# Mamba steps that alternate over both halves of the channels, with a gather in two 128x64 products and DRAM reads that repeat 64 rows

## The chip, the cores and the metric

The kernel runs on one core of one Trainium2 chip. The metric is the device time of one execution in microseconds (us); before the change it is 8173.62 us, the median of three runs (8168.15 to 8188.78). A core has five engines that run on their own queues: PE (matrix products, into the accumulator memory PSUM), DVE (VectorE), ACT (ScalarE), POOL (GpSimd) and SP, which only issues transfers. Transfers are carried out by 16 DMA engines.

## The reference

Four layers run one after the other on an image x of 2 x 64 channels x 96 x 96, all in float32. Layer 0 is attention over the 9216 points of each image. Layer 1 is a depthwise and a pointwise convolution and one Mamba block over the 9216 points as one sequence. Layer 2 runs four Mamba blocks: forward and backward along one image axis, then forward and backward along the other, over sequences of 96. Layer 3 is a 3x3 filter whose taps are computed from the image's means. The change is in the Mamba block, of which this is the core:

```python
dt, Bm, Cm = jnp.split(dbc, [DT_RANK, DT_RANK + D_STATE], axis=-1)
dt = jax.nn.softplus(jnp.einsum('blr,dr->bld', dt, dt_proj_w) + dt_proj_b)
A = -jnp.exp(A_log)
dA = jnp.exp(dt[..., None] * A)
dBx = dt[..., None] * Bm[:, :, None, :] * xc[..., None]

def step(hc, inp):
    dA_t, dBx_t, C_t = inp
    hc = hc * dA_t + dBx_t
    y = jnp.einsum('bds,bs->bd', hc, C_t)
    return (hc, y)
...
ys = (ys + xc * Dp) * jax.nn.silu(z)
```

There are 128 inner channels d and 16 states s: 2048 recurrences run beside each other along the time l.

## The kernel before, in words

**Units and steps.** The work of layers 1 and 2 is cut into 120 units of 768 columns of time (`CH`): 24 in layer 1 (12 for each image, one after the other in time, with the last state carried on in `u.carry`), and 96 in layer 2 (8 sequences of 96 in each, forward or backward, no carry). A unit has 16 steps (`STEPS`), since 128 partitions hold 128 of the 2048 recurrences at a time (16 of them for all 768 columns, or 32 half as long), and so there are 1920 steps.

**Which recurrence lies where.** In step n, partition p works on state p // 8 and on channel (p + 8n) mod 128. After 16 steps each channel has met all 16 states. To bring the channels to their partitions, a unit writes its 128 rows of dt and dt*x (`u.both`, 1536 columns) to DRAM twice, one below the other (`step_write`, L824, two transfers of 768 KB), into `rows` of 256 x 1536. A step then reads 128 rows from row 8n on (`read`): that is a turn by 8n.

**Two forms of a step.** In layer 1 a step reads one transfer of 768 KB (L842), for all 768 columns of one group of channels n. In layer 2 (`u.paired`) a step takes one half of the time, 384 columns, for two neighbouring groups 2m and 2m + 1, side by side in the free dimension, and reads them with two transfers of 384 KB (L847). The rest of a step:

- `decay` on ACT: exp(rate * dt) into `h`, one activation of 768 columns (L853) or two of 384 (L857), since the rate differs between groups.
- `shared` on PE: B for all partitions (L866), into a bank that all steps of the unit (or of a half of its time) read.
- `inputs` on DVE: dt*x times B into a `place` in PSUM (L872, L877). In layer 2 those of two steps come together, ahead of an even step.
- `scan` on DVE: the recurrence along 768 columns (L884 with the carried state, L890 without: there a decay of zero at the start of each sequence resets it). POOL then multiplies by C (L886, L893), and in layer 1 copies the last state (L885).
- `gather` on PE: a 128x128 matrix of zeros and ones (`t.gather[n]`) adds the 128 rows of `h` to their channels. Layer 1 adds columns 0 to 383 into the bank `low0` and the others into `low1`; layer 2 adds both groups into `low1` (L910), 3840 products in all, each standing as two records in the profile. The product with `direct` (L907), ahead of the first, puts the term with Dp there.

**The order.** `run` writes the order out by hand. In iteration n SP gets the reads of step n + 5 (`READ`), ACT the decay of step n + 3, DVE the inputs and scan of step n, PE the gather of a step two back (`lates`), and then those parts of earlier or later units whose offsets in `PIECES` fall on n: norm, convolution, gate, dt, C ahead of the unit, and the reading of y and the output projection behind it. `step_write` stands at -8, so between the reads of steps -3 and -2 of its unit. `spread`, the tile that a read fills, has six buffers, and `h` nine. `y_half` and `y_read` (L915, L919, L923) copy the finished halves of y from PSUM. Between the last unit of layer 1 and the first of layer 2 the form changes, and a branch gathers and reads out y at once (`u.drained`).

**Tables.** `mamba_tables` builds the matrices of the gather (`pair`, two identities side by side, of which 16 windows are taken) and, with `turned`, what `mamba_weights` needs to put the rates of each step in its order. This runs during attention.

Of the kernel before, what the change touches and what calls it, by code (L numbers as in the profile page):

```python
# [523 lines left out]
def mamba_tables(k, pool):  # L524

    nc = k.nc
    G = P // 8
    t = SimpleNamespace()  # L530

    t.member = pool.tile([P, 8], FP, name="member")
    nc.vector.reduce_sum(t.member, k.ident.rearrange("p (g i) -> p i g", i=8), axis=AX.X)
    t.group = pool.tile([P, 2, G], FP, name="group")
    for j in range(2):
        nc.vector.reduce_sum(t.group[:, j], k.ident.rearrange("p (g i) -> p g i", i=8), axis=AX.X)

    t.turned = pool.tile([P, G, G], FP, name="turned")
    two = t.group.rearrange("p j g -> p (j g)")
    for n in range(G):  # L540
        nc.vector.tensor_copy(t.turned[:, n], two[:, G - n : 2 * G - n])

    pair = pool.tile([P, 2, P], FP, name="pair")
    nc.vector.tensor_copy(pair, k.ident.unsqueeze(1).to_broadcast([P, 2, P]))
    pair = pair.rearrange("p j c -> p (j c)")
    t.gather = [pair[:, P - 8 * n : 2 * P - 8 * n] for n in range(G)]

    t.centre = pool.tile([P, P], FP, name="centre")
    nc.vector.tensor_sub(t.centre, k.ident, k.mean_c)
    return t  # L550
# [8 lines left out]
def mamba_weights(k, w, pool, product, tables, i):  # L559
# [15 lines left out]
    p = product(tables.placed.rearrange("p s i -> p (s i)"), tables.group[:, 0], P, G)  # L575
# [38 lines left out]
class Mamba:  # L614
# [14 lines left out]

    STEPS = P // 8  # L630
# [3 lines left out]
    def __init__(self, k, tables, wk, dram, ps, ps_m):  # L634
        self.k, self.nc, self.t = k, k.nc, tables
        self.wk, self.dram, self.ps_m = wk, dram, ps_m


        self.places = [self.wide(ps.tile([P, 2 * NB], FP, name=f"place{i}")) for i in range(2)]
        self.low = [ps.tile([P, NB], FP, name=f"low{i}")[:, :HALF] for i in range(2)]  # L640
# [141 lines left out]
    def step_read(self, u):  # L782
        nc = self.nc

        u.both = self.work("dtu", 2 * CH, bufs=1)
        order = "p (j a t) -> p a j t" if u.paired else "p (a j t) -> p a j t"
        both = u.both.rearrange(order, a=2, j=2)
        u.dt, u.e = both[:, 0], both[:, 1]
        u.kept = self.by_half(self.work("kept", bufs=1))
        p = self.by_half(u.p)  # L790
        nc.scalar.activation(u.e, p, AF.Abs, bias=u.w.dt_b)
        nc.scalar.activation(u.dt, p, AF.Relu, bias=u.w.dt_b)
# [28 lines left out]
    def step_write(self, u):  # L821
        u.rows = self.dram.tile([2 * P, 2 * CH], FP, tag="rows", name="rows")
        for j in range(2):
            self.nc.sync.dma_start(out=u.rows[j * P : (j + 1) * P], in_=u.both)  # L824
# [10 lines left out]
    def paired(self, step):  # L835
        half, m = divmod(step, self.STEPS // 2)
        return half, (2 * m, 2 * m + 1)

    def read(self, u, step):
        u.dtu[step] = self.work("spread", 2 * CH, bufs=6)  # L840
        if not u.paired:
            self.nc.sync.dma_start(out=u.dtu[step], in_=u.rows[8 * step : 8 * step + P])  # L842
            return
        half, groups = self.paired(step)
        for q, n in enumerate(groups):
            row = u.rows[8 * n : 8 * n + P, bass.ts(half, CH)]
            self.nc.sync.dma_start(out=u.dtu[step][:, bass.ts(q, CH)], in_=row)  # L847

    def decay(self, u, step):

        h = u.h[step] = self.work("h", bufs=9)
        if not u.paired:
            self.nc.scalar.activation(h, u.dtu[step][:, :CH], AF.Exp, scale=u.w.rates[:, step : step + 1])  # L853
            return
        for q, n in enumerate(self.paired(step)[1]):
            dt = u.dtu[step][:, q * CH : q * CH + HALF]
            self.nc.scalar.activation(h[:, bass.ts(q, HALF)], dt, AF.Exp, scale=u.w.rates[:, n : n + 1])  # L857

    def shared(self, u, half=0):

        if u.paired:
            sides, halves = [self.low[0]], [half]
        else:
            (sides, u.B), halves = self.places[1], range(2)
        for j, p in zip(halves, sides):
            self.nc.tensor.matmul(p, lhsT=u.w.bc[0], rhs=u.xc[:, bass.ts(j, HALF)], start=True, stop=True)  # L866

    def inputs(self, u, step):

        if not u.paired:  # L870
            u.bx = self.places[0][1]
            self.nc.vector.tensor_mul(u.bx, u.dtu[step][:, CH:], u.B)  # L872
            return
        bx = self.places[step % 2][1].rearrange("p (q t) -> p q t", q=2)
        x = u.dtu[step].rearrange("p (q a t) -> p q a t", q=2, a=2)[:, :, 1]
        B = self.low[0].unsqueeze(1).to_broadcast([P, 2, HALF])
        self.nc.vector.tensor_mul(bx, x, B)  # L877

    def scan(self, u, step):
        nc = self.nc  # L880
        h = u.h[step]
        if not u.paired:
            first = u.carry[:, step : step + 1]
            nc.vector.tensor_tensor_scan(h, h, u.bx, first, ALU.mult, ALU.add)  # L884
            nc.gpsimd.tensor_copy(first, h[:, CH - 1 :])  # L885
            nc.gpsimd.tensor_mul(h, h, u.C)  # L886
            return
        bx = self.places[step % 2][1]
        way = slice(None, None, -1) if u.rev else slice(None)
        nc.vector.tensor_tensor_scan(h[:, way], h[:, way], bx[:, way], 0.0, ALU.mult, ALU.add)  # L890
        h = h.rearrange("p (q t) -> p q t", q=2)
        C = u.C[:, bass.ts(self.paired(step)[0], HALF)]
        nc.gpsimd.tensor_mul(h, h, C.unsqueeze(1).to_broadcast([P, 2, HALF]))  # L893

    def gather(self, u, step):

        if u.paired:
            half, groups = self.paired(step)
            parts = [(half, self.low[1], q, n) for q, n in enumerate(groups)]
            begin, end = step % 8 == 0, step % 8 == 7  # L900
        else:
            parts = [(j, p, j, step) for j, p in enumerate(self.low)]
            begin, end = step == 0, step == self.STEPS - 1
        h = u.h[step]
        if begin:
            for half, p in {half: p for half, p, _, _ in parts}.items():
                self.nc.tensor.matmul(p, lhsT=u.w.direct, rhs=u.xc[:, bass.ts(half, HALF)], start=True, stop=False)  # L907
        for i, (_, p, q, n) in enumerate(parts):
            stop = end and (i == 1 or not u.paired)
            self.nc.tensor.matmul(p, lhsT=self.t.gather[n], rhs=h[:, bass.ts(q, HALF)], start=False, stop=stop)  # L910

    def y_half(self, u):
        if u.paired:
            u.y = self.work("yg")
            self.nc.scalar.copy(u.y[:, :HALF], self.low[1])  # L915

    def y_read(self, u):
        if u.paired:
            self.nc.scalar.copy(u.y[:, HALF:], self.low[1])  # L919
        elif not u.drained:  # L920
            u.y = self.work("yg")
            for j, p in enumerate(self.low):
                self.nc.scalar.copy(u.y[:, bass.ts(j, HALF)], p)  # L923
# [65 lines left out]
    @staticmethod  # L989
    def lates(now, s):  # L990
        halves = now and now[0].paired
        if s == 2 or (s == 10 and halves):
            return ()
        if s == 3 or (s == 11 and halves):
            return (3, 2)
        return (2,)

    def run(self, units, first, n_first, other):


        for u in units:
            u.dtu, u.h, u.paired, u.drained = {}, {}, not u.carry, False
# [5 lines left out]
        unit = lambda i: units[i] if i < len(units) else None  # L1008
# [16 lines left out]
        for n in range(begin, len(steps) + end + 1):  # L1025
# [5 lines left out]
            if at(n):  # L1031
# [3 lines left out]
                if not u.paired:  # L1035
                    self.inputs(u, s)
                elif s % 2 == 0:
# [3 lines left out]
                if u.paired and s == 6:  # L1041
                    self.shared(u, 1)
                if s == (14 if u.paired else 15) and unit(n // self.STEPS + 1):
                    after = unit(n // self.STEPS + 1)
                    if after.paired and not u.paired:

                        for late in (2, 1, 0):
                            self.gather(u, s - late)
                        self.y_read(u)
                        u.drained = True  # L1050
                    self.shared(after)
            if n == -1:
                self.shared(units[0])

            for late in self.lates(at(n), s):
                if at(n - late) and not (at(n - late)[0].drained):
# [297 lines left out]
```

## Time and profile before

| | |
|---|---|
| runs | 8168.15, 8173.62, 8188.78 us |
| the profiled execution: its time, its span | 8176.64, 8174.9 us |
| granted TensorE clock, mean | 0.955 |
| attention (layer 0) | until about 2713 us, almost no transfers |
| layer 1 | about 1229 us, 24 units, 51.2 us each |
| layer 2 | about 4138 us, 96 units, 43.1 us each |
| layer 3 | about 95 us |
| read from and written to DRAM | 1522.68 and 197.79 MB |

The span reaches from the first to the last instruction of the profiled execution. "Busy" is the time in which an engine works on an instruction; products on PE overlap each other, so that their busy time says more than it holds PE. The stages have different limits, and an average over the span can mislead: what a change is worth is read from its own stage. These are the largest groups of POOL, VectorE and ScalarE in the steps of layer 2 (columns: line, engine, operation, written and read tiles, shapes, count; then busy us, mean ns of one; then the engine's idle time ahead of them and what ended it):

```profile
L893 POOL TENSOR_TENSOR h<-h,C 128x768 f32<-128x768 f32 x1536 | 2755.1, 1819 | 231.7 <-DVE h L890 225.1
L890 DVE TENSOR_TENSOR_SCAN h<-h,place 128x768 f32<-128x768 f32 x1536 | 2604.3, 1737 | 4.9 <-ACT h L857 4.9
...
L857 ACT ACTIVATE h<-spread,xa 128x384 f32<-128x384 f32 x3072 | 1717.2, 607 | 368.7 <-DMA spread<-rows 336.8
L877 DVE TENSOR_TENSOR place<-spread,low 128x768 f32<-128x768 f32 x1536 | 1388.3, 949 | 251.0 <-PE low L866 238.4
```

### The profile page before, as it was taken

The page shows a single profiled execution, that of the slowest core. Times are in us where ns is not written, and L with a number is a line of the kernel's source. Part 1 is how long each engine was busy: PE and PEld are TensorE (multiplying, and loading weights), DVE is VectorE, ACT ScalarE, POOL GpSimd, SP SyncE. Part 2 cuts the span into 40 slices and gives each one's busy share as a digit, 9 for nine tenths or more (in the row PEclk, how much of TensorE's full clock was granted, in tenths as well). Part 3 has the DMA queues.
Part 4 walks back from the last instruction along what each step waited for, and adds up shares of the span by engine and source line. Part 5 has one row for each costly group of instructions (what it writes and reads, how often), then busy time and mean ns, then how long its engine had stood idle before and what let it go on. Part 6 is the DMA issues. An engine that isn't in the chain of part 4 may idle for free.

```text
span 8174.9 us, 80364 instructions
## 1 busy us (share of the span) xinstructions
PE 7554.5 (92%) x24578; PEld 3358.0 (41%) x24578; DVE 6785.6 (83%) x5136; ACT 5045.4 (62%) x6473; POOL 4755.1 (58%) x3146
## 2 busy tenths in 40 slices
PE   9999999999999799999889998989999999999897
PEld 3333333333333344444444444444444444444443
DVE  6666666666666599988899999999999999999999
ACT  4444444444444566665676677777777777777774
POOL 0000000000000588888888888898999989888895
PEclk9999999999999798988999999999999999999999
DMA  1000000000000588777888888888898888888885
GB/s 42 1 1 1 1 1 1 3 4 4 4 4 5 205 294 296 284 286 277 292 315 317 317 321 333 330 324 331 334 337 328 330 336 336 331 321 334 324 329 211
DMA packets 538496, 1725.90 MB, mean 211 GB/s; under 512 B 59844, under 2 KB 60996, under 8 KB 537544
## 3 DMA queue, kind: packets, MB, share of 16 engines
q1 hardware_dynamic: 536608, 1717.66, 56.8%
q8 instruction: 194, 3.18, 0.2%
q10 hardware_dynamic: 1448, 3.05, 0.1%
q14 instruction: 246, 2.02, 0.1%
HBM read 1522.68 MB, written 197.79 MB: 210 GB/s over the span
## 4 chain that ended last, share of the span: by engine, by line
PE 21%; POOL 13%; issue 12%; ACT 8%; DMA 8%; DVE 4%; SPq 0%; DVEq 0%; ACTq 0%; POOLq 0%
PE low L910 10%; DMA spread<-rows 6%; POOL h L886 5%; POOL h L893 4%; PE mm L666 4%; ACT h L857 4%; PE conv L754 4%; DVE place L877 2%; DMA rows<-dtu 1%; PE low L907 1%; PE conv L748 1%; DVE h L890 1%; POOL dtu L811 1%; PE low L866 1%; ACT raw L773 1%
## 5 line engine op out<-in xcount | busy, mean ns | idle before, releaser
L910 PE MATMUL low<-h,pair 128*128 128x384 f32 x7680 | 2865.4, 515 | 44.2 <-POOL h L886 26.5
L893 POOL TENSOR_TENSOR h<-h,C 128x768 f32<-128x768 f32 x1536 | 2755.1, 1819 | 231.7 <-DVE h L890 225.1
L890 DVE TENSOR_TENSOR_SCAN h<-h,place 128x768 f32<-128x768 f32 x1536 | 2604.3, 1737 | 4.9 <-ACT h L857 4.9
L910 PEld LDWEIGHTS low<-h,pair 128*128 128x128 f32 x7680 | 1503.2, 201 | 1288.6 <-issue 270.7
L307 ACT ACTIVATE e<-f_exp 128x1536 f32<-128x1536 f32 x864 | 1207.1, 1449 | 1223.7 <-PE f_exp L297 1223.7
L363 DVE TENSOR_TENSOR acc_e<-acc_e,e 128x1536 f32<-128x1536 f32 x792 | 1389.9, 1755 | 684.5 <-ACT e L307 645.2
L857 ACT ACTIVATE h<-spread,xa 128x384 f32<-128x384 f32 x3072 | 1717.2, 607 | 368.7 <-DMA spread<-rows 336.8
L877 DVE TENSOR_TENSOR place<-spread,low 128x768 f32<-128x768 f32 x1536 | 1388.3, 949 | 251.0 <-PE low L866 238.4
L336 POOL TENSOR_TENSOR xa<-xa,t_att 64x512 f32<-64x512 f32 x36 | 45.4, 1261 | 2612.4 <-ACT t_att L334 2612.4
L314 PE MATMUL y_att<-e,xb 128*64 128x512 f32 x5184 | 1243.6, 601 | 0.0
L297 PE MATMUL f_exp<-theta,phi 64*128 64x512 f32 x5184 | 1234.4, 606 | 1.0 <-DVE xb L280 0.5
L297 PEld LDWEIGHTS f_exp<-theta,phi 64*128 64x128 f32 x5184 | 466.2, 186 | 754.6 <-issue 460.8
L884 DVE TENSOR_TENSOR_SCAN h<-h,state,place 128x768 f32<-128x768 f32 x384 | 696.1, 1813 | 67.7 <-ACT h L853 19.2
L886 POOL TENSOR_TENSOR h<-h,C 128x768 f32<-128x768 f32 x384 | 695.3, 1811 | 31.4 <-POOL state L885 1.0
L314 PEld LDWEIGHTS y_att<-e,xb 128*64 128x64 f32 x5184 | 341.5, 136 | 830.7 <-issue 829.3
L765 ACT ACTIVATE raw<-conv,cols 128x768 f32<-128x768 f32 x120 | 108.2, 901 | 886.1 <-PE conv L754 587.0
L754 PE MATMUL conv<-xn,xa 64*128 64x384 f32 (+3 forms) x1536 | 557.9, 503 | 16.6 <-DVE xa L1128 5.3
L872 DVE TENSOR_TENSOR place<-spread,place 128x768 f32<-128x768 f32 x384 | 369.1, 961 | 129.3 <-PE place L866 116.9
L853 ACT ACTIVATE h<-spread,rates 128x768 f32<-128x768 f32 x384 | 351.1, 931 | 175.0 <-DMA spread<-rows 173.6
L907 PE MATMUL low<-raw,xa 128*128 128x384 f32 x384 | 220.2, 662 | 257.8 <-ACT yg L915 175.6
L754 PEld LDWEIGHTS conv<-xn,xa 64*128 64x128 f32 x1536 | 277.6, 190 | 286.7 <-issue 98.7
L805 POOL TENSOR_TENSOR kept<-dtu,kept 128x768 f32<-128x768 f32 x120 | 218.2, 1819 | 285.1 <-ACT kept L798 285.1
(207 smaller groups left out, 6041.4 us busy)
## 6 DMA issues: line engine op xcount, KB each, us to landing
spread<-rows SPq DMA_DIRECT2D x3072, 384.0 KB, 6.4
spread<-rows SPq DMA_DIRECT2D x384, 768.0 KB, 4.5
rows<-dtu SPq DMA_DIRECT2D x240, 768.0 KB, 5.8
image<-pre SPq DMA_DIRECT2D x11, 384.0 KB, 2.3
xb<-image SPq DMA_DIRECT2D x11, 384.0 KB, 7.9
xa<-in_x SPq DMA_DIRECT2D x1, 2304.0 KB, 22.2
out<-xa ACTq DMA_DIRECT2D x7, 240.0 KB, 2.0
out<-xa SPq DMA_DIRECT2D x1, 1200.0 KB
```

What stands on the lines that cost most here:

```text
L297: nc.tensor.matmul(fs[j // 3][:, bass.ts(j % 3, NB)], lhsT=phi[at, bass.ts(m // 2, P)], rhs=theta[at, bass.ts(i, NB)], start=True, stop=True,)
L307: nc.scalar.activation(e, f, AF.Exp)
L314: nc.tensor.matmul(y[rows_of(m % 2)], lhsT=g[:, m, :], rhs=es[j // 3][:, bass.ts(j % 3, NB)], start=m < 2, stop=m >= KEYS - 2,)
L363: nc.vector.tensor_add(acc, acc, e)
L754: self.nc.tensor.matmul(p3[:, :, o], lhsT=lhsT, rhs=x3[:, :, i], **flags)
L857: self.nc.scalar.activation(h[:, bass.ts(q, HALF)], dt, AF.Exp, scale=u.w.rates[:, n : n + 1])
L877: self.nc.vector.tensor_mul(bx, x, B)
L884: nc.vector.tensor_tensor_scan(h, h, u.bx, first, ALU.mult, ALU.add)
L886: nc.gpsimd.tensor_mul(h, h, u.C)
L890: nc.vector.tensor_tensor_scan(h[:, way], h[:, way], bx[:, way], 0.0, ALU.mult, ALU.add)
L893: nc.gpsimd.tensor_mul(h, h, C.unsqueeze(1).to_broadcast([P, 2, HALF]))
L910: self.nc.tensor.matmul(p, lhsT=self.t.gather[n], rhs=h[:, bass.ts(q, HALF)], start=False, stop=stop)
```

## The change

All 120 units now take one form of step. A step covers one half of the time (384 columns: steps 0 to 7 the first, 8 to 15 the second) and one turn of 0 to 7, and it takes one group of rows from each half q of the channels (0 to 63, 64 to 127). Partition p, with c = p mod 64, holds channel 64q + (c + 8 * turn) mod 64 and state p // 8 in the columns of half q.

- **Write.** Each half's 64 rows go to DRAM twice, one below the other: four transfers of 64 rows instead of two of 128.
- **Read.** For each half one transfer takes 64 rows, and an axis of two with step 0 repeats them for partitions 64 to 127. Layer 1 now reads as layer 2 does, two transfers of 384 KB for each of 16 steps.
- **Gather.** The 128x128 matrices become 128x64; the product of half q goes to its 64 rows of one bank `y`. The bank `B` takes the place of `low0`.
- **Layer 1.** Two activations for a step's decay, two scans of 384 columns with a state each, and one copy of both states. B and y are made and read out for one half of the time at a time, as in layer 2. The branch between the layers goes.
- **Tables.** `turned`, `pair` and the windows follow the new order.

```diff
     def step_write(self, u):
         u.rows = self.dram.tile([2 * P, 2 * CH], FP, tag="rows", name="rows")
-        for j in range(2):
-            self.nc.sync.dma_start(out=u.rows[j * P : (j + 1) * P], in_=u.both)
+        for q in range(2):
+            for at in range(q * P, (q + 1) * P, C):
+                self.nc.sync.dma_start(out=u.rows[at : at + C], in_=u.both[rows_of(q)])
...
+    def turn(step):
+        return divmod(step, Mamba.STEPS // 2)

     def read(self, u, step):
+        half, turn = self.turn(step)
         u.dtu[step] = self.work("spread", 2 * CH, bufs=6)
-        if not u.paired:
-            self.nc.sync.dma_start(out=u.dtu[step], in_=u.rows[8 * step : 8 * step + P])
-            return
-        half, groups = self.paired(step)
-        for q, n in enumerate(groups):
-            row = u.rows[8 * n : 8 * n + P, bass.ts(half, CH)]
-            self.nc.sync.dma_start(out=u.dtu[step][:, bass.ts(q, CH)], in_=row)
+        for q in range(2):
+            at = q * P + 8 * turn
+            rows = u.rows[at : at + C, bass.ts(half, CH)].unsqueeze(0).to_broadcast([2, C, CH])
+            self.nc.sync.dma_start(out=u.dtu[step][:, bass.ts(q, CH)], in_=rows)
...
     def scan(self, u, step):
...
+        if u.carry:
+            state = u.carry[:, 2 * turn : 2 * turn + 2]
+            for q in range(2):
+                at = bass.ts(q, HALF)
+                nc.vector.tensor_tensor_scan(h[:, at], h[:, at], bx[:, at], state[:, q : q + 1], ALU.mult, ALU.add)
+            nc.gpsimd.tensor_copy(state.unsqueeze(2), h2[:, :, HALF - 1 :])
+        else:
+            way = slice(None, None, -1) if u.rev else slice(None)
+            nc.vector.tensor_tensor_scan(h[:, way], h[:, way], bx[:, way], 0.0, ALU.mult, ALU.add)
...
     def gather(self, u, step):
...
+        half, turn = self.turn(step)
+        if turn == 0:
+            self.nc.tensor.matmul(self.y, lhsT=u.w.direct, rhs=u.xc[:, bass.ts(half, HALF)], start=True, stop=False)
+        for q in range(2):
+            rhs, stop = u.h[step][:, bass.ts(q, HALF)], turn == self.STEPS // 2 - 1
+            self.nc.tensor.matmul(self.y[rows_of(q)], lhsT=self.t.gather[turn], rhs=rhs, start=False, stop=stop)
...
-    pair = pool.tile([P, 2, P], FP, name="pair")
-    nc.vector.tensor_copy(pair, k.ident.unsqueeze(1).to_broadcast([P, 2, P]))
+    pair = pool.tile([P, 2, C], FP, name="pair")
+    for j in range(2):
+        nc.vector.tensor_add(pair[:, j], k.ident[:, :C], k.ident[:, C:])
     pair = pair.rearrange("p j c -> p (j c)")
-    t.gather = [pair[:, P - 8 * n : 2 * P - 8 * n] for n in range(G)]
+    t.gather = [pair[:, C - 8 * n : 2 * C - 8 * n] for n in range(T)]
```

## The prediction

> **What bounds the kernel now.** I read four views, in this order: the totals, the stretches, the waits of the stretch that holds most of the time, and the DMA tables, since the change alters every transfer of the long part. First the totals of the page.
>
> ```profile
> span 8174.9 us, 80364 instructions
> PE 7554.5 (92%) x24578; PEld 3358.0 (41%) x24578; DVE 6785.6 (83%) x5136; ACT 5045.4 (62%) x6473; POOL 4755.1 (58%) x3146
> ```
>
> PE looks like the bound, but the stages differ. The stretches show attention up to 2713 us, layer 1 to 3942, layer 2 to 8080, then layer 3 (columns: stretch, length, busy us and count of PE, PEld, DVE, ACT, POOL, granted clock, DMA share, GB/s).
>
> ```profile
> 2713.00:3942.00 1229.00, 1120.62 (x2861) 528.03 (x2860) 1075.57 (x799) 766.69 (x888) 1013.57 (x936) 0.90 0.77 281
> 3942.00:8080.00 4138.00, 3738.49 (x10315) 1905.05 (x10313) 3883.00 (x3100) 2981.01 (x4597) 3670.57 (x2146) 0.95 0.88 328
> ```
>
> In layer 2 VectorE is busy 3883 of 4138 us (94%) and the transfers stand at 0.88 of all 16 DMA engines: two limits close together. The VectorE waits of that stretch say what ends last, and they are small:
>
> ```profile
> DVE place L877 <- PE low L866: 238.4, 99, 5.2
> DVE place L877 <- DMA spread<-rows: 12.0, 20, 1.0
> ```
>
> Only 12 us of 4138 are lost to a late read. The reads are on time because they are spread over 16 engines. The DMA issues, and the same table for the first 50 us alone:
>
> ```profile
> spread<-rows SPq DMA_DIRECT2D x3072, 384.0 KB, 6.4
> spread<-rows SPq DMA_DIRECT2D x384, 768.0 KB, 4.5
> rows<-dtu SPq DMA_DIRECT2D x240, 768.0 KB, 5.8
> ```
>
> ```profile
> DMA packets 1227, 8.45 MB, mean 169 GB/s; under 512 B 196, under 2 KB 452, under 8 KB 840
> ...
> q10 hardware_dynamic: 440, 1.33, 11.0%
> ...
> mats<-in_mats ACTq DMA_DIRECT2D x1, 1058.0 KB, 12.4
> mats<-in_mats ACTq DMA_DIRECT2D x1, 160.0 KB, 2.4
> cols<-in_cols ACTq DMA_DIRECT2D x1, 71.5 KB, 4.7
> dtw<-in_dtw ACTq DMA_DIRECT2D x1, 10.0 KB
> ```
>
> Here is what decides this forecast. Queue q10 carried four loads: three of 128 rows and dtw of 4 rows. Their row packets are 3 x 128 + 4 = 388, and 440 - 388 = 52 are left, which is 3 x 16 + 4. Thirteen loads began in this window; 12 x 16 + 4 = 196 is also exactly the count under 512 B. So each transfer ends with one small packet per engine that took part: 16 for 128 or 64 rows, and 4 for the 4-row one. **The number of engines follows the outermost count of the transfer.**
>
> **The change, part by part.** *The read.* Each of the 1920 steps (120 units x 16) now issues two reads whose DRAM side is 2 copies x 64 rows x 768 elements: its outermost count is 2, while the SBUF side has 128 partitions. No row here has a 2 against a 128. The bounds are 16 engines (nothing lost) and 2 engines. The nearest row is dtw, where a small outermost count gave just as many engines, and I take 2. Nor can the trace tell which engines a short transfer takes; the ends are always the same pair, or pairs in turn. One short load can't show a moving start, so this is a choice and no reading: I take the same pair, the split that starts at the first engine each time, and keep the other as a rival.
>
> One engine then moves 64 packets of 3072 B per read. What one packet costs is read where only such packets fly: the reload of the image before layer 1, two stretches.
>
> ```profile
> 2668.00:2670.00 2.00, 0.73 (x3) 0.06 (x1) 0.00 (x0) 1.11 (x2) 0.00 (x0) 0.87 1.01 378
> 2670.00:2672.00 2.00, 1.52 (x3) 0.72 (x4) 0.00 (x0) 0.38 (x1) 0.00 (x0) 0.50 1.02 410
> ```
>
> The last gives 410 / (16 x 1.02) = 25.1 GB/s per engine, 122 ns per packet; the one before 131 ns. The image stores of layer 0, which fly alone, give the lower end (1408 row packets at 0.9% of 16 engines from 1500 to 2650 us: 117 ns); layer 2 at 89.0% over 5000 to 7000 us gives the upper (28,480 engine-us for 204,070 row packets: 140 ns, larger writes included). With two engines little competes, so I take 122.
>
> A read is 64 x 0.122 + 0.009 = 7.8 us, a step 15.6 us, against about 2.6 us per step in layer 2 now (4138 / 1536 = 2.69). 1920 x 15.63 = 30,020 us. The six spread buffers and a lead of five steps cannot help: they fill the queue of the pair, they don't widen it. SP then stands at each read until a spread buffer comes free, and the writes queue behind it; every engine is late by the same reads, and nothing else can be late next.
>
> *The write.* Four transfers of 64 partitions per unit instead of two of 128, the same bytes. 64 rows gave 16 engines above. The pair carries 4 x 4 rows of 6144 B per unit behind its reads: 16 x 0.245 = 3.9 us, x 120 = 470 us. Its issue stands on SP between the reads of steps -3 and -2. Read 0 of the next unit waits for it, and is then still covered by two queued steps (31 us), so no hole opens.
>
> *The gather.* 3840 products (two records each) of 128x128x384 become 128x64, the two of a step on separate halves of one bank. On the queue now:
>
> ```profile
> L910 PE MATMUL low<-h,pair 128*128 128x384 f32 x7680 | 2865.4, 515 | 44.2 <-POOL h L886 26.5
> L314 PE MATMUL y_att<-e,xb 128*64 128x512 f32 x5184 | 1243.6, 601 | 0.0
> ```
>
> L314 already runs 128x64 products on alternate halves: in the timeline 12 records of 512 columns take 2.79 us, 0.23 us each, while 24 records of L910 with 384 columns take 7.90 us, 0.33 each. Per column that is 0.45 against 0.86 ns, so side by side works, and a step's gather falls from 1.32 to about 0.70 us: some 1190 us of PE time over 1920 steps. What it can be worth in time is bounded by the PE waits of VectorE, 238 us in layer 2. Behind reads of 15.6 us per step it is worth nothing.
>
> *Layer 1 in the same steps.* Its 384 steps get two activations of 607 ns for one of 931 (+109 us on ACT), two scans of 384 for one of 768 (1813 ns; no row has the short one: between nothing and 0.15 us more, the price of the small VectorE instructions at the start, so 0 to 58 us), and one state copy as before. All of it is hidden when a step waits 15.6 us; without that cover it is set against the 137 us that VectorE waits there, 88 of them at the start. The branch that drained layer 1 before layer 2 goes. Setup gains a few VectorE instructions of 0.2 us under attention.
>
> **Sum.** The first read goes out at 2713 us as now; 30,020 of reads, 470 of writes, and from the last landing to the end 94 us as now: 33,300 us. The profiled execution had a span of 8174.9, a time of 8176.6, the runs a median of 8173.6; the 3 us don't matter here.
>
> [...]
>
> **The rivals.** *The pattern is not confined (the change does what it says):* if the lowering puts the row axis outermost, reads stay at 16 engines and the bytes are the same. For it: the very same 384 KB transfers run well now. Against it: dtw. Then VectorE stays the bound, and the faster gather returns perhaps half of the 238 us, layer 1 some 50 of its 137: about 8000 us, faster.
>
> *Confined, but pairs take turns:* up to 12 reads are in flight, 8 pairs give 8 reads per 7.8 us, about 1.0 per us against 0.75 needed (2 per 2.69 us). This nearly fits the lead of five steps (13 us against 7.8 of data plus the 2 us by which the quickest read's 3.0 us exceed its own data); where reads bunch behind a write it does not, and I put 0.2 us on each step: 8000 + 1920 x 0.2 = 8400 us, slower. It decides from the point where a read lands later than 13 us after its issue. Nothing in the trace speaks for turns.
>
> *Reads stay wide, but the split scan of layer 1 lengthens its chain:* at twice my upper end, 0.3 us on 384 steps, 115 us against the gains of 170: 8120 us, still faster. It can't carry the sign.
>
> **How the numbers follow.** Confined to one pair 0.83; not confined, with either scan price, 0.12; pairs in turn 0.05. The forecast is 33,300 us. Its range comes from the packet: 117 ns gives 28,800 + 450 + 2810 = 32,000, 140 ns gives 34,400 + 540 + 2810 = 37,800. I take 31,800 to 37,800, which holds nearly all of the 0.83. The other cases lie at 8000 to 8400 and are left out. A measurement of this kernel tells about 0.3% from no change: slower 0.87, same 0.02, faster 0.11.
>
> **What would show it.** Confined: the DMA share in layers 1 and 2 is about 2/16, 0.12 to 0.13, at about 50 GB/s; reads take some 80 us or more to land, since five steps queue on the pair; ACT waits on spread for most of the span; and the packets under 512 B fall from 59,844 to about 16,000 (3840 reads x 2 + 480 writes x 16 + some 700 others). If they come out near 70,000 the reads ran on 16 engines and the forecast is wrong. With 16,000 and a share well above 0.13, pairs take turns. The gather is right if the four records of a step take about 0.7 us at full clock, or twice that at the granted 0.50 that the two stretches of the reload show where PE has little to do.

## The result, and the profile after

The changed kernel takes 32,930.5 us, the median of four runs (32,928.3 to 32,934.0), against 8181.2 us for the kernel before in four runs of the same series (8168.2 to 8192.4): 4.025 times as long, with a 95% interval of 4.018 to 4.033. The prediction was 33,300 us, slower, and the time lies in its range.

First the totals of the page of the changed kernel, in the order in which they were read before.

```profile
span 32926.4 us, 82385 instructions
PE 8638.1 (26%) x24578; PEld 2952.2 (9%) x24578; DVE 6917.5 (21%) x5523; ACT 5379.3 (16%) x6857; POOL 4755.7 (14%) x3146
...
DMA packets 543887, 1725.87 MB, mean 52 GB/s; under 512 B 16068, under 2 KB 17220, under 8 KB 542920
```

VectorE, ScalarE and POOL have about as much to do as before (6785.6, 5045.4 and 4755.1 us), in a span four times as long: no engine is the bound. The bytes are the same too, 1725.9 MB. What fell is the number of small packets, from 59,844 to 16,068. The prediction had "about 16,000"; the page's number is exactly 2 for each of 3840 reads, 16 for each of 480 writes, and 708 others (as many as the kernel before has beside 16 for each of its 3696 reads and writes). So each read ran on two engines, and each write of 64 rows on 16.

A stretch in the middle of layer 2 (columns as before: stretch, length, busy us and count of PE, PEld, DVE, ACT, POOL, granted clock, DMA share, GB/s):

```profile
9200.00:20000.00 10800.00, 2086.70 (x4682) 716.76 (x4682) 1807.91 (x1405) 1455.62 (x2067) 1660.18 (x967) 0.55 0.15 57
```

A share of 0.15 is 2.4 of 16 engines. A unit takes about 250 us. Its 4096 row packets of 3072 B took 124 ns each on average, 508 us of engine time or 2.03 engines: the pair is full. The other 0.42 engine is the writes: 256 packets of 6144 B at 408 ns on average. The prediction's 0.12 to 0.13 left the writes out, and its own price of them, 245 ns, would have added only 0.25 engine.

The waits of ScalarE and VectorE over the whole span (us in total, times, longest):

```profile
ACT h L859 <- DMA spread<-rows: 25974.1, 3831, 10.5
DVE place L869 <- DMA spread<-rows: 24025.0, 1858, 15.5
```

The wait for late reads was 12 us in layer 2 before, and is 24,025 us now, in nearly all of the 1920 steps. ScalarE's timeline shows the rhythm (start, duration, instruction; in brackets the idle time before it and what ended it):

```profile
20026.51 0.61 ACT L859 ACTIVATE h<-spread,xa 128x384 f32<-128x384 f32 x1 [7.06 <-DMA spread<-rows]
...
20034.28 0.62 ACT L859 ACTIVATE h<-spread,xa 128x384 f32<-128x384 f32 x1 [5.61 <-DMA spread<-rows]
20041.94 0.61 ACT L859 ACTIVATE h<-spread,xa 128x384 f32<-128x384 f32 x1 [7.04 <-DMA spread<-rows]
20049.72 0.61 ACT L859 ACTIVATE h<-spread,xa 128x384 f32<-128x384 f32 x1 [7.16 <-DMA spread<-rows]
```

One activation for each read, every 7.66 to 7.78 us; where a write lies between two reads, 11.4 us. The sum from these rows: start 2715, 3840 reads x 7.7 = 29,570, 120 writes x 3.7 = 440, tail 94, together 32,820 us, within 0.4% of the span.

### The profile page after: what moved, and what is told of

Its sections match the earlier page's. It is cut to its first block, busy times and chain, and to the rows that moved or that the text cites. A ratio compares the mean times of both kernels' runs of the same rounds, so it can differ in the third digit from the quotient of the medians.

```text
span 32926.4 us, 82385 instructions
## 1 busy us (share of the span) xinstructions
PE 8638.1 (26%) x24578; PEld 2952.2 (9%) x24578; DVE 6917.5 (21%) x5523; ACT 5379.3 (16%) x6857; POOL 4755.7 (14%) x3146
## 4 chain that ended last, share of the span: by engine, by line
DMA 77%; SPq 11%; ACT 3%; issue 0%; DVE 0%; PE 0%; POOL 0%; DVEq 0%; POOLq 0%
DMA spread<-rows 77%; SPq L850 11%; ACT h L859 2%; ACT kept L802 0%; ACT kept L801 0%; ACT dtu L800 0%; DVE xa L1217 0%; ACT yg L898 0%; ACT yg L901 0%; ACT xn L738 0%; PE mm L671 0%; PE conv L753 0%; DMA xb<-image 0%; DMA rows<-dtu 0%; DVE xb L190 0%
## 5 line engine op out<-in xcount | busy, mean ns | idle before, releaser
L869 DVE TENSOR_TENSOR place<-spread,B 128x768 f32<-128x768 f32 x1920 | 1847.2, 962 | 24595.1 <-DMA spread<-rows 24025.0
L894 PE MATMUL y<-h,pair 128*64 128x384 f32 x7680 | 2393.5, 767 | 28.2 <-POOL h L885 28.2
L891 PE MATMUL y<-raw,xa 128*128 128x384 f32 x384 | 316.3, 927 | 6536.0 <-ACT yg L901 4132.5
L671 PE MATMUL mm<-xn,mats 64*128 64x384 f32 x480 | 350.9, 884 | 4315.5 <-ACT raw L770 4315.5
L859 ACT ACTIVATE h<-spread,rates 128x384 f32<-128x384 f32 x768 | 471.8, 614 | 5122.5 <-DMA spread<-rows 5089.8
L863 PE MATMUL B<-raw,xa 128*128 128x384 f32 x384 | 316.3, 927 | 3278.8 <-DVE place L869 3278.8
L671 PE MATMUL mm<-raw,xa 128*128 128x384 f32 x768 | 511.5, 815 | 1948.4 <-ACT dtu L796 1183.6
L759 PE MATMUL conv<-xn,xa 64*128 64x384 f32 (+3 forms) x1536 | 830.1, 702 | 378.6 <-ACT sq L715 374.7
L894 PEld LDWEIGHTS y<-h,pair 128*64 128x64 f32 x7680 | 682.8, 204 | 1688.2 <-issue 1541.3
L880 DVE TENSOR_TENSOR_SCAN h<-h,state,place 128x384 f32<-128x384 f32 x768 | 714.4, 992 | 0.0
```

What stands on the lines that cost most here:

```text
L671: self.nc.tensor.matmul(o, lhsT=lhsT, rhs=x, start=n == 0, stop=n == len(terms) - 1)
L759: self.nc.tensor.matmul(p3[:, :, o], lhsT=lhsT, rhs=x3[:, :, i], **flags)
L869: self.nc.vector.tensor_mul(bx, x, self.B.unsqueeze(1).to_broadcast([P, 2, HALF]))
L894: self.nc.tensor.matmul(self.y[rows_of(q)], lhsT=self.t.gather[turn], rhs=rhs, start=False, stop=stop)
```

## The experiments

The edits are against the changed kernel, unless another is named. In each series the kernel before ran on the same chip; it had medians of 8175 to 8187 us.

### How many engines: copies4 and copies16

The read repeats 32 rows four times, or 8 rows sixteen times, in place of 64 rows twice.

```diff
-            rows = u.rows[at : at + C, bass.ts(half, CH)].unsqueeze(0).to_broadcast([2, C, CH])
+            rows = u.rows[at : at + P // 4, bass.ts(half, CH)].unsqueeze(0).to_broadcast([4, P // 4, CH])
```

> The changed kernel, but each read takes 4 copies of 32 rows instead of 2 copies of 64 (the same 128 partitions and bytes; most channels get other rows, so dt and dt*x are not those of the reference). Theory A (the number of engines is the outermost count of the pattern, the same engines each time): 4 engines, 32 packets each, 32 x 0.121 + 0.009 = 3.88 us a read, 7.76 us a step; 1920 x 7.76 + 450 of writes + 2810 = 18,200 us (17,800 to 18,800); DMA share about 0.28. Rival B (the repetition itself is slow: a step of 0, or rows that are read twice at the same time): no faster than the 32,930 us of the change, rather slower, since each row is now read four times. Completion packets under 512 B: A 3840 x 4 + 480 x 16 + 708 = 23,748.

Measured: 18,161.9 us in one run, and 23,748 small packets. The stretch of layer 2, columns as above:

```profile
4000.00:17000.00 13000.00, 4785.27 (x11150) 1644.84 (x11146) 4307.64 (x3539) 3447.20 (x4948) 3965.85 (x2518) 0.60 0.30 111
```

Share and rate are twice those of the changed kernel (0.15 and 57 GB/s). The reading itself repeats as before, and only the outermost count went from 2 to 4. In these two kernels the count set the number of engines: 23,748 small packets are 4 for each of 3840 reads, 16 for each of 480 writes and the same 708 others. That repeating in itself holds the changed kernel back is out, since 4 copies took 18,161.9 us and 2 took 32,930.5.

> As the 4-copies kernel, but 16 copies of 8 rows in each read (again other rows than the reference's). Theory A: 16 engines, so the reads are as wide as before the change and VectorE is the bound again: about 8000 us (7900 to 8200), DMA share in layer 2 about 0.88, packets under 512 B 69,828. Rival B (repetition is slow): 32,930 us or more, each row being read 16 times.

Measured: 8955.3 us in one run, not 8000. The page of this kernel, the DMA totals and the queue of the reads (packets, MB, share of 16 engines' span):

```profile
DMA packets 597647, 1726.08 MB, mean 193 GB/s; under 512 B 69828, under 2 KB 70980, under 8 KB 596680
...
q1 hardware_dynamic: 595744, 1717.70, 70.9%
```

69,828 is 3840 x 16 + 480 x 16 + 708: all 16 engines took part, as expected. But the same bytes that took 56.8% of 16 engines in the kernel before, over a span of 8175 us, take 70.9% here over 8954. A packet of 3072 B took 187 ns (median), against 121 before. The engines are all there, and each packet takes longer. This was not foreseen. Whether it comes from the places that each engine writes, or from sixteen readers of the same eight rows, no run separates.

### Whether wide reads make the change fast: two_reads and three_copies

The first replaces the repeating read by two plain reads of 64 rows; the second writes each half's 64 rows three times, so that a plain read of 128 rows does it.

```diff
-            rows = u.rows[at : at + C, bass.ts(half, CH)].unsqueeze(0).to_broadcast([2, C, CH])
-            self.nc.sync.dma_start(out=u.dtu[step][:, bass.ts(q, CH)], in_=rows)
+            rows = u.rows[at : at + C, bass.ts(half, CH)]
+            for j in range(2):
+                self.nc.sync.dma_start(out=u.dtu[step][rows_of(j), bass.ts(q, CH)], in_=rows)
```

> The changed kernel with each repeating read split into two plain reads of 64 rows into 64 partitions, the same rows twice; all results as in the reference. Theory A: 64 rows on both sides give 16 engines: 8000 us (7900 to 8150), with 4 reads of 192 KB a step and about 1.4 us of SP's time for them. Rival B, in its form that reading the same DRAM rows twice at once is slow: about 32,900; in its form that the step of 0 is slow: 8000 too, so that only the 16-copies kernel tells it from A. If the faster gather is worth nothing with wide reads: 8175.

Measured: 9291.2 us (9269.8 to 9308.6), 1.136 times before (1.134 to 1.139). The reads ran on 16 engines, which were full (1.02 from 4000 to 9000 us) at only 265 GB/s, and their packets took 191 ns (median).

```diff
-        u.rows = self.dram.tile([2 * P, 2 * CH], FP, tag="rows", name="rows")
+        u.rows = self.dram.tile([6 * C, 2 * CH], FP, tag="rows", name="rows")
         for q in range(2):
-            for at in range(q * P, (q + 1) * P, C):
+            for at in range(3 * q * C, 3 * (q + 1) * C, C):
                 self.nc.sync.dma_start(out=u.rows[at : at + C], in_=u.both[rows_of(q)])
...
-            at = q * P + 8 * turn
-            rows = u.rows[at : at + C, bass.ts(half, CH)].unsqueeze(0).to_broadcast([2, C, CH])
+            at = q * 3 * C + 8 * turn
+            rows = u.rows[at : at + P, bass.ts(half, CH)]
```

> The changed kernel with the 64 rows of each half written three times, one below the other (6 writes of 64 rows a unit instead of 4), so that 128 rows from row 8 x turn on are the repeated 64, and one plain read of 128 rows takes the place of the repeating one; all results as in the reference. Theory A: 16 engines: 8000 us (7900 to 8150). It carries 720 KB x ... no: 768 KB more of writes per unit (2 x 384 KB), 16 x 3 us of one engine's 43 us, so where the transfers were at 0.88 they come to about 0.92; if they become the bound it is above two_reads, otherwise equal. Rival B: 8000 too, no row is read twice by one transfer.

Measured: 8906.8 us (8897.9 to 8917.2), 1.088 times before (1.086 to 1.091). Here the reads have the form of the kernel before, and their packets took 121 ns again (median). What differs is the writes: SP's issue of them in the timeline (start, duration, instruction), and two stretches of 2 us in which they fly (columns as above).

```profile
6024.60 8.04 SPq L829 DMA_DIRECT2D rows<-dtu  x6
```

```profile
6026.00:6028.00 2.00, 0.34 (x4) 0.00 (x0) 2.00 (x2) 1.98 (x2) 2.00 (x2) 1.00 0.96 203
6028.00:6030.00 2.00, 0.00 (x0) 0.00 (x0) 2.00 (x3) 1.98 (x2) 2.00 (x2) 1.00 0.96 200
```

The same two views of the kernel before, where the writes have 128 rows:

```profile
5510.02 0.80 SPq L824 DMA_DIRECT2D rows<-dtu  x2
```

```profile
5512.00:5514.00 2.00, 1.73 (x6) 0.71 (x4) 2.00 (x2) 1.99 (x2) 2.00 (x2) 1.00 1.05 393
5514.00:5516.00 2.00, 0.00 (x0) 0.00 (x0) 2.00 (x3) 1.97 (x3) 1.92 (x2) 1.00 0.94 221
```

The engines are nearly all busy in all four stretches. The writes of 64 rows move some 200 GB/s; those of 128 rows move 393, but 221 in their last part. So the price is not simply double: over layer 2 a packet of 6144 B took 446 ns on average in three_copies (median 472), and 299 in the kernel before (median 245). Nor do 64 rows set it alone. The writes of copies16 are the same 64-row writes as the changed kernel's, and there such a packet took 234 ns (median); from 6009 to 6011 us, when 133 of the 145 row packets that began were a write's, the transfers stood at 427 GB/s and a share of 1.03. Why these writes reach that rate in copies16, no run shows.

SP stands 8.04 us at its six writes, and the reads behind them go out late. VectorE waited 935 us for late reads in three_copies.

### The narrow writes alone: before_narrow

Against the kernel before; the two writes of 128 rows are cut into four of 64, with the same bytes at the same place, and nothing else.

```diff
         for j in range(2):
-            self.nc.sync.dma_start(out=u.rows[j * P : (j + 1) * P], in_=u.both)
+            for q in range(2):
+                at = j * P + q * C
+                self.nc.sync.dma_start(out=u.rows[at : at + C], in_=u.both[rows_of(q)])
```

> The kernel before with one part of the change alone: each of its two writes of 128 rows is cut into two of 64 rows (same bytes, same places; results as in the reference). Theory N (why the kernels with wide reads are at 8900 to 9300 and not at 8000: a transfer with 64 partitions on the SBUF side moves at half the rate; its 6144-byte packets took 472 ns in the three-copies kernel against 235 before): 16 packets an engine and unit, 3.8 us more of all engines' time per unit, and the reads queue behind: between nothing and 450 us more, I expect 8450 (8250 to 8650). Rival D (the loss lies in the new steps themselves, the gather, the banks or layer 1's form): 8175, no change.

Measured: 8459.6 us (8453.6 to 8466.1), 1.033 times before (1.031 to 1.035). The narrow writes cost some 273 us by themselves, at an unchanged number of bytes (and of engines, if they ran on 16 as the changed kernel's writes did): the four writes hold SP 4.00 us in the timeline, where two took 0.80, and VectorE's wait for late reads goes from 12 us to 280. The edit also doubles the number of transfers, and no run separates the two; that the packets themselves got longer (from 4000 to 8300 us 356 ns on average, against 299 in layer 2 before) speaks for the width.

### The rest of the change with full transfers: wide, wide_whole, even_odd

Three copies of all 128 rows, written in three transfers, and a read that takes every second row from row 16 x turn + q on: the halves are then the even and the odd channels, and every transfer has 128 partitions. In wide and wide_whole the tables were left for the old halves, so that channels are mixed; the work is the same. even_odd has the tables, weights and columns for these halves too.

```diff
-        u.rows = self.dram.tile([2 * P, 2 * CH], FP, tag="rows", name="rows")
-        for q in range(2):
-            for at in range(q * P, (q + 1) * P, C):
-                self.nc.sync.dma_start(out=u.rows[at : at + C], in_=u.both[rows_of(q)])
+        u.rows = self.dram.tile([3 * P, 2 * CH], FP, tag="rows", name="rows")
+        for j in range(3):
+            self.nc.sync.dma_start(out=u.rows[j * P : (j + 1) * P], in_=u.both)
...
-            at = q * P + 8 * turn
-            rows = u.rows[at : at + C, bass.ts(half, CH)].unsqueeze(0).to_broadcast([2, C, CH])
+            rows = u.rows.rearrange("(c q) t -> c q t", q=2)[8 * turn : 8 * turn + P, q, bass.ts(half, CH)]
```

> The changed kernel with both transfers at full width: the 128 rows written three times by three transfers of 128 rows, and each read one plain transfer of 128 rows that takes every second row (so a half of the channels is the even or the odd ones; rates, gather and C's order are left as they are, so channels are mixed up and the output is not the reference's). Theory N: no transfer has less than 128 partitions, so nothing is left against the gains: 8050 us (7950 to 8175), packets of 6144 bytes at about 240 ns. Rival D: the new steps cost what they cost in the three-copies kernel, about 8900.

Measured: 8201.5 us (8189.2 to 8209.9), 1.0020 times before (1.0009 to 1.0031). The 25,000 us are gone, but the faster gather and layer 1 bring nothing in sum. From the start of the first scan of a layer to that of its last, layer 1 took 1141 us (before 1182) and layer 2 took 4218 (before 4148). The waits of VectorE in layer 2, from 3950 to 7900 us:

```profile
DVE place L867 <- DMA spread<-rows: 208.9, 159, 2.8
DVE place L867 <- PE B L861: 65.2, 59, 2.6
```

In the kernel before, the same stretch has 225.0 us for PE and 11.0 for late reads. The wait for PE was indeed taken away, and the wait for reads stands in its place.

The next run takes the gather back to whole 128x128 products and leaves the rest of wide as it is; they add both halves into one result, which changes what is computed.

```diff
-            self.nc.tensor.matmul(self.y[rows_of(q)], lhsT=self.t.gather[turn], rhs=rhs, start=False, stop=stop)
+            self.nc.tensor.matmul(self.y, lhsT=self.t.pair, rhs=rhs, start=False, stop=stop and q == 1)
```

> As the wide kernel, but each product of the gather takes a whole 128x128 matrix (two shifted identities side by side, so both halves of y get the sum of both; not the reference's output) into all 128 rows of the bank, as before the change: the side-by-side products are taken away and all else stays. If the faster gather is worth something: slower than wide by up to the 238 us that VectorE waited for PE in layer 2; I expect 100 more. If PE is well hidden: the same as wide within 30 us.

Measured: 8221.4 us (8205.0 to 8226.8), 1.0043 times before (1.0029 to 1.0058): the gather side by side is worth about 20 us here, no more than the runs of one kernel lie apart. The stretch of layer 2 in wide, and then in wide_whole:

```profile
3942.00:8080.00 4138.00, 3137.64 (x10187) 1153.17 (x10186) 3827.61 (x3046) 2951.81 (x4535) 3617.02 (x2115) 0.85 0.90 340
```

```profile
3942.00:8080.00 4138.00, 3691.07 (x10090) 1875.20 (x10089) 3789.44 (x3014) 2930.53 (x4492) 3583.92 (x2097) 0.94 0.90 337
```

PE is busy 550 us less with the narrow products, at a granted clock of 0.85 against 0.94; how much time the lower clock costs was not measured by itself. From 3950 to 7900 us VectorE waits 199.4 us for PE and 124.9 for reads in wide_whole, against 65.2 and 208.9 in wide: as the one wait goes, the other grows.

The sum over both layers hides something. By the scans of these two executions, layer 2 takes 4218 us in wide and 4257 in wide_whole, but layer 1 takes 1141 in wide and 1104 in wide_whole, where the clock in layer 1 is 0.82 and 0.98. So the narrow products gain some 40 us in layer 2 and lose nearly as much in layer 1. This rests on one execution of each kernel, and why layer 1 loses stays open.

> The wide kernel made whole: the two halves of the channels are the even and the odd ones in every table, in the direct term, in the gate's columns and in the rows of the output projection, so that the results are the reference's. The instructions are those of wide but for a few small ones under attention: 8200 us (8180 to 8230). Rival: a longer start of layer 1, 8210 to 8260.

Measured: 8202.1 us (8192.2 to 8208.5), 1.0023 times before (1.0012 to 1.0035). The tables for these halves cost nothing that can be seen.

### The wait for reads: lead6, write7, before_write7

Two ways to get the reads out earlier in even_odd: one step more of lead (with `spread` of seven buffers, and `h` of seven to make room), or the write one step later in the hand-written order. In the kernel before a write holds SP until POOL has made `dtu` (L819; 703.5 us in 91 waits from 3950 to 7900 us), and the reads queue behind it.

```diff
-    READ = 5
+    READ = 6
...
-        u.dtu[step] = self.work("spread", 2 * CH, bufs=6)
+        u.dtu[step] = self.work("spread", 2 * CH, bufs=7)
...
-        h = u.h[step] = self.work("h", bufs=9)
+        h = u.h[step] = self.work("h", bufs=7)
```

> As even_odd, with the reads six steps ahead instead of five, seven spread buffers and, to make room, seven h buffers instead of nine. Theory E (in wide VectorE's wait for PE in layer 2 fell from 238 to 65 us, and its wait for reads rose from 12 to 222, because the third copy lengthens the write that the reads queue behind): a step more of lead, 2.6 us, covers most of those waits (183 of them, none over 2.8 us): 8030 us (7980 to 8100). Rival F (the transfers themselves are full, 0.90 of 16 engines): no gain, 8200. Rival G (seven h buffers hold ScalarE up, since a decay three steps ahead then waits for a gather three steps back): 8250 or more.

Measured: 8039.7 us (8029.7 to 8049.3), 0.9823 times before (0.9807 to 0.9840).

```diff
-        (-8, "step_write"),
+        (-7, "step_write"),
```

> As even_odd, with the write one step later in the order (between the reads of steps -2 and -1 instead of -3 and -2), so that SP holds back one read less while it waits for POOL. Theory E: one more step's reads are out before the write; the first read of the unit then has 2.6 us less between the write and its own issue, which the write's 4.8 us of landing may take back: 8120 us (8050 to 8250). Rival F: 8200.

Measured: 8032.4 us (8026.3 to 8040.8), 0.9820 times before (0.9803 to 0.9837): more than was expected, from one number. Since the move has nothing to do with the change, it was then made alone, in the kernel before.

> The kernel before with the one move of write7 alone (the write at -7 instead of -8). It tells whether the gain of write7 belongs to the new steps or to the move. Theory E (before, VectorE waits 12 us for reads and 238 us for PE in layer 2; only the faster gather makes the reads the next limit): no gain, 8185 us (8160 to 8210), or a little slower, since the unit's first read is closer to the write. Rival H (the move helps by itself): 8030 to 8100.

Measured: 8082.6 us (8079.4 to 8093.6), 0.9881 times before (0.9861 to 0.9900). The expectation of no gain was wrong. The queue's own waits on SP from 3950 to 7900 us in the kernel before, then VectorE's and SP's in before_write7:

```profile
SPq L824 <- POOL dtu L819: 703.5, 91, 10.0
```

```profile
DVE place L877 <- PE low L866: 154.1, 74, 4.3
```

```profile
SPq L824 <- POOL dtu L819: 315.3, 94, 4.2
```

SP stood 704 us at its writes, up to 10.0 us each time, and stands 315 us now. VectorE's wait for PE, 225.0 us in this stretch before, fell to 154 though nothing of PE's work was changed, and its wait for reads is no longer in the table. So a move on SP's queue took away about a third of the wait that the profile put down to PE in the kernel before. That its root was late reads, which came to PE by way of work standing late ahead of B, is a reading, which no run shows by itself.

What is left of the change's own worth is the difference between write7 and before_write7, some 50 us (two series, each against its own runs of the kernel before). By the first and last scans, layer 1 takes 1123 against 1182 us, 59 less, and layer 2 takes 4062 against 4050, 12 more. The waits of VectorE in write7 from 3950 to 7900 us, and its stretch of layer 2:

```profile
DVE place L876 <- PE B L870: 107.9, 81, 2.7
DVE place L876 <- DMA spread<-rows: 33.8, 59, 1.8
```

```profile
3890.00:7900.00 4010.00, 3106.48 (x10237) 1143.84 (x10238) 3840.07 (x3066) 2946.26 (x4552) 3640.42 (x2131) 0.86 0.94 353
```

The transfers are at 0.94 of 16 engines and 353 GB/s, in before_write7 at 0.92 and 334: three copies written instead of two leave less room. That this takes back what the gather gains in layer 2 is argued from these rows; a version with wide reads and only two copies was not tried.

### The same pair: two_queues

Back to the changed kernel: the reads of the second half are issued from ScalarE's queue, with the outermost count of 2 as it is.

```diff
-            self.nc.sync.dma_start(out=u.dtu[step][:, bass.ts(q, CH)], in_=rows)
+            queue = self.nc.scalar if q else self.nc.sync
+            queue.dma_start(out=u.dtu[step][:, bass.ts(q, CH)], in_=rows)
```

> The changed kernel with the reads of the second half of the channels issued by ScalarE's queue instead of SP's; results as in the reference. Theory A with the same engines each time (a transfer of outermost count 2 starts at the first engine whatever the queue): both queues fill the same pair, 32,900 us (32,600 to 33,400). Rival C (the pair depends on the queue or goes in turn): two pairs share the reads, about 2810 + 15,000 + 450 = 18,200 us.

Measured: 32,943.0 us in one run. The queues on the page (packets, MB, share of 16 engines' span):

```profile
q1 hardware_dynamic: 292384, 962.49, 8.4%
...
q10 hardware_dynamic: 251048, 758.04, 5.8%
```

Half of the reads did move to the other queue, and the time did not change; from 4000 to 30,000 us the share was 0.15 at 56 GB/s, against 0.15 and 57 in the changed kernel. So the reads of both queues shared the same two engines here; for different pairs the expectation had an estimate of 18,200 us.

## Why the prediction was right, point by point

- **The bound before.** VectorE and the transfers were close together, as read. The wait for PE was taken at its word, though: moving one write, with PE's work untouched, removed a third of it.
- **Outermost count and engines.** Right. 2, 4 and 16 copies gave 2, 4 and 16 engines by the small packets, each to the packet, and 32,930, 18,162 and 8955 us. The row of dtw, one load of four rows, was enough to see it.
- **The same pair, not turns.** A choice in the prediction. The share of 0.15 and two_queues settle it against turns. Which two engines they are can't be seen in the records, so a split that starts at the first engine, as the prediction chose it, was not shown; that the reads kept to one pair was.
- **The read.** 7.82 us predicted. From ScalarE's use of the first read (2743.5 us) to that of the last (32,840.5), less 440 us for the writes, a read took 7.73 us on average. Over 3840 reads that is some 350 us less, most of the 370 by which the forecast was too high. The 117 ns of the range's lower end comes from a share rounded to 0.9%; those 1408 packets took 122 ns on average in the trace. The sign that reads take "some 80 us or more to land" was wrong. These are SP's issues of the reads (ns min/median/max, first and last start in us):

```profile
L850 SPq DMA_DIRECT2D spread<-rows x3840: 519/7506/14001, 2715.1 to 32813.7; - x192
```

An issue alone holds SP 7.5 us at the median (0.37 before), all of them together 28,412 us, and the last read is used 27 us after its issue began. So two or three reads stand on the pair at a time, not ten, and what holds SP is mostly the issue itself, not the wait for a spread buffer that the prediction named. The sum does not depend on it, since the pair is full either way.
- **The write: right on the pair, too cheap beside it.** It was priced at 16 x 0.245 = 3.9 us of the pair's time per unit, and the hole in the reads is 3.7, so the term of the sum holds. But 245 ns was the packet of a transfer of 128 rows, and the step took for granted that 64 rows on 16 engines cost the same. Over the stretch of layer 2 above, a quarter of these packets took up to 241 ns, half 465 or more. In the changed kernel this lies beside the pair and costs nothing. In before_narrow the narrow writes cost 273 us, and 64-row transfers are most of why the rival "not confined" was too low: its 8000 us became 9291 and 8907, and 8202 with full transfers. In the stretches of three_copies the writes of 64 rows moved 200 to 203 GB/s, where those of 128 moved 393 in the kernel before. The 427 GB/s of copies16 and the 221 at the end of a 128-row write do not follow from the number of rows alone, and the cause was not shown.
- **The gather.** The four records of a step take 2393.5 / 1920 = 1.25 us at a granted 0.55. At full clock that would be 0.69 if the time went with the clock, an estimate; 0.70 was predicted. In write7, at a granted 0.86 in layer 2, they take 1743.1 / 1920 = 0.91 us. Of the two stretches of the reload, one shows the 0.50 that the prediction named, with PE busy 1.52 of 2 us; the other shows 0.87, with 0.73. The gather is worth nothing behind the reads, as said. With full transfers it brings 20 us, where half of 238 was allowed for in the rival: reads took over the wait in layer 2, and layer 1 got longer by nearly as much as layer 2 got shorter.
- **Layer 1.** The split scan was priced at 0 to 0.15 us more for each step. This is the group of the changed kernel (columns: line, operation, shapes, count; busy us, mean ns; idle time before):

```profile
L880 DVE TENSOR_TENSOR_SCAN h<-h,state,place 128x384 f32<-128x384 f32 x768 | 714.4, 992 | 0.0
```

Two of 992 ns against one of 1813 is 0.17 us more, 66 us over 384 steps, a little above the upper end. Layer 1 is still 37 (lead6) to 78 us (wide_whole) shorter in the kernels with full transfers, around the 50 of the rival.
- **The rival that the split scan decides** was out: no kernel with full transfers shows a longer layer 1. With 64-row transfers or 16 copies it is 90 to 110 us longer, but the narrow writes alone lengthen it by 52 in before_narrow, with the scans as they were.

## What to carry to other kernels

Read a transfer's outermost count before its bytes: here a repeated axis of 2 or 4 in front left 2 or 4 of 16 DMA engines for the reads, and the transfers moved 57 and 111 GB/s, where the kernel before moved 328 in layer 2. Try a transfer with all 128 partitions as well as all 16 engines: in before_narrow four writes of 64 rows cost 273 us against two of 128. A full share of busy engines at few GB/s is a sign to look at how it is cut (200 GB/s with 64 rows, 281 with 16 copies of 8 rows, each at a share of 0.96 or more). Before a faster engine is built, look at what stands on SP's queue: a write that waited there for its data (703.5 us from 3950 to 7900 us) held back the reads behind it, and moving it by one step gained more (1.2%) than the halved gather and the new layer 1 together (0.6%). The best version that was run, even_odd with the write moved (write7), takes 8032 us, 0.982 times the kernel before.

## What the runs showed of the hardware that was not expected

- Writes of 64 rows on 16 engines ran at half the rate of writes of 128 in the stretches of three_copies and the kernel before, 200 against 393 GB/s, and a packet of 6144 B took 446 against 299 ns on average over layer 2. In copies16 they reached 427 GB/s.
- Reads were slower with all engines and all 128 partitions too: with 16 copies of 8 rows a packet of 3072 B took 187 ns (median) against 121, and from 4000 to 8700 us the transfers stood at a share of 1.03 with 281 GB/s. The cause was not shown.
- The issue of a transfer itself held SP: 7.5 us at the median for a read on two engines, 3.7 on four (copies4), 0.37 for a read of 384 KB in the kernel before, on 16.
- The granted clock was lower with the narrower products: in layer 2 0.95 before and 0.94 in wide_whole (PE busy 3691 of 4138 us), 0.85 in wide (3138), and 0.55 in the changed kernel, where PE is busy 2086.7 of 10,800 us. A step's gather kept PE busy 1.25 us there, against 1.49 us with the wide products of the kernel before (2865.4 / 1920).
